# A decoder layer on one core: six of eight block transposes move from TensorE to VectorE and DMA, with a new order of token rows

## The chip, the cores and the metric

One Trainium2 chip, one of its cores. The core has a TensorE (matrix products into PSUM), a VectorE, a ScalarE and a GpSimd, and DMA queues that its engines issue to; SyncE (SP) issues most of the transfers here. The metric is the device time of one execution in microseconds. An execution that was profiled apart from the timed ones gives the profile.

## The reference, cut to what matters

2048 tokens of 512 features go through grouped self-attention against 512 gathered cache rows and the keys of the first sequence, cross attention against an encoder output within each sequence of 64 tokens, and a feed-forward with a low-rank part. After each, the result is added to the tokens and normalised.

```python
# x: (32, 64, 512); 32 query heads, 8 key/value heads, head dimension 128
k_full = concatenate([k_cache[block_idx], k[0]])        # 512 + 64 keys, the same for all tokens
x = layernorm(x + softmax(q @ k_full.T / sqrt(128)) @ v_full @ wo.T)
q = x @ Wq + bq
k, v = split(ctx @ Wkv + bkv)                            # 64 keys in each sequence
x = layernorm(x + softmax(q @ k.T / sqrt(128)) @ v @ Wo + bo)
z = x @ W.T + b
m = sum over e of p[e] * (x @ A[e]) @ B[e]
x = layernorm(x + z + min(0.5 * |z| / (|m| + 1e-6), 1) * m)
```

Everything is float32. In self-attention each token meets the same 576 keys, so neither the order of the tokens nor that of the keys matters there. In cross attention a token must meet the 64 keys of its own sequence.

## The kernel before

**Blocks.** The tokens are cut into four blocks (`NTB`) of 512 (`TB`). A block lives in two forms. `acc[tb]`, 128 partitions by 4 rows (`TPB`) by 512 features, collects the sums and is normalised in place: tokens lie on partitions. `xT[tb]`, 128 partitions by 4 feature groups by 512 tokens, feeds the products: features lie on partitions. `rows` (L113) says which token stands where in `acc`: row j of partition p is token 128 j + p of the block. The columns of `xT` run in token order.

**Turning a block.** Twice an `acc` block has to be turned into an `xT` block, after the first and after the second normalisation. `transpose_rows` (L127) does one row of 128 tokens: four TensorE transposes of 128x128 into one bank of PSUM (L131) and one copy out by ScalarE or VectorE in turn (L133).

**Stages.** (1) Self-attention, a loop over 128 units, with its products, VectorE reductions and 32x32 turns of the weights. At its start the queries of block 0 and `new_keys` (L586, keys and values of the first 64 tokens) come from `xTs[0]`; later groups read a copy of its first 64 columns, `x64`, that GpSimd makes at L812. (2) The key/value stage, a loop over pairs `(gp, tb)` of two key/value heads and a block; each pair has seven products ("steps"). Between steps one closure of the list `fill` runs: the parts of the first normalisation (put there at gp 1) and then `rows_turn`, a row's `transpose_rows` (put there at gp 2). Each pair ends with two stores of keys and values to DRAM. (3) Cross attention, a loop over 32 units `(g, tb)`. Iteration n makes the queries of unit n (seven steps), then `attend(n - 1)`, then the scores of unit n, then the seven steps of the output projection of unit n - 1 (`steps`), with the softmax of unit n between them (`parts`). (4) The feed-forward of a block (`feed_forward`), the first two interleaved with the last units.

**The products of stage 3.** Each product of two 512-wide matrices is done by seven products of halves, some of them of sums of halves. `attend` (L1128) writes its PSUM banks to `oTx`, tokens on the free axis, four copies of 128x256 on ScalarE (L1161) and four on VectorE (L1163). `output_sums` (L262) lets GpSimd form four sums of the halves of `oTx` (L267 to L273). In `project` the first step needs no sum; the second, step 5, needs the sum of L267, the third, step 6, that of L268.

**Order.** TensorE and VectorE follow the order that is written out in stages 2 and 3, GpSimd too in stage 3; VectorE's order is free from the last full unit on. Each engine takes its instructions in order, so an instruction that waits holds back all that stand behind it. SP issues its transfers in one queue, in order as well.

**The end of stage 3.** When a block's last projection is done (g is 7), its normalisation runs (`layernorm_parts` with ScalarE scaling the rows, L169), and `later` holds `transpose_block` (L135), 16 transposes. For blocks 0 and 1 it runs one iteration after that projection, ahead of query step 4 of the last two full units; for blocks 2 and 3 it runs beside the feed-forward. `feed_forward` takes 128 columns of `xT[tb]` at a time as weights (`cols`, L1212), adds to row i of `acc`, normalises it and stores it.

Of the kernel before, what the change touches and what calls it, by code (L numbers as in the profile page):

```python
# [9 lines left out]
F32 = mybir.dt.float32  # L10
I32 = mybir.dt.int32
AF = mybir.ActivationFunctionType
ALU = mybir.AluOpType
# [39 lines left out]
def decoder_layer(  # L53
# [46 lines left out]


    acc = [act.tile([P, TPB, DIM], F32, tag=f"acc{b}", name=f"acc{b}") for b in range(NTB)]
    xT = []
# [9 lines left out]
    def rows(src, tb):  # L113
        return src[tb * TB : (tb + 1) * TB, :].rearrange("(j p) f -> p j f", p=P)

# [19 lines left out]
    def transpose_block(tb, name):  # L135
        for j in range(TPB):
            transpose_rows(acc[tb][:, j, :], xT[tb], j, f"{name}_{tb}_{j}")

    def layernorm(tb, name):
# [344 lines left out]
    with ExitStack() as ph:  # L484
# [81 lines left out]
        def rotate(g, t0=0, t1=NKT):  # L566
# [15 lines left out]
            nc.vector.tensor_tensor(k4[:, :, :, 0], k4[:, :, :, 0], tmp, ALU.add)  # L582

        x64 = kc.tile([P, NC, SEQ], F32, name="x64")

        def new_keys(g):  # L586

            wk, wv = wkv_cur.pop(g)  # L590
            src = xTs[0] if g == 0 else x64
            kTs[g] = kv.tile([P, NKEY], F32, tag="kT", name=f"kT{g}")
            new = bank([P, 1, TB], f"new{g}", "po1")[:, 0, :]
            pk, pv = new[:, :SEQ], new[:, P : 2 * P]
            for c in range(NC):
                nc.tensor.matmul(
                    pk, wk[:, c, :], src[:, c, :SEQ], start=(c == 0), stop=(c == NC - 1),
                    skip_group_check=True,
                )
            for c in range(NC):  # L600
                for i in range(2):
                    nc.tensor.matmul(
                        pv[i * SEQ : (i + 1) * SEQ, :], src[:, c, :SEQ], wv[:, c, :],
                        start=False, stop=(c == NC - 1), skip_group_check=True,
                    )
# [175 lines left out]
        for j in range(NKT):  # L781
            gather_keys(0, j)
        nc.vector.tensor_tensor(t[1], q[0, 1], q[0, 0], sub)
        nc.vector.tensor_tensor(wq0[7], wq0[1], wq0[5], sub)
# [26 lines left out]
        cached_keys(0, "s0")  # L811
        nc.gpsimd.tensor_copy(x64, xTs[0][:, :, :SEQ])  # L812
        nc.vector.tensor_tensor(t[3], q[1, 1], q[0, 1], sub)
# [153 lines left out]
    with ExitStack() as ph:  # L967
# [23 lines left out]
        with ExitStack() as st:  # L991
# [8 lines left out]
            kvw[1] = load_kv_left(1, "wo")  # L1000
            fill, turns = [], [0]

            def rows_turn(src, dst, j, name):
                transpose_rows(src, dst, j, name, f"t{turns[0] % 2}")
                turns[0] += 1

            pairs = [(gp, tb) for gp in range(NKV // 2) for tb in range(NTB)][1:]
            for k, (gp, tb) in enumerate(pairs):
# [3 lines left out]
                if gp == 2:  # L1012
                    fill += [lambda tb=tb, j=j: rows_turn(
                        acc[tb][:, j, :], xT[tb], j, f"x1_{tb}_{j}") for j in range(TPB)]
                tiles = [ke.tile([P, 2, 2, HF], F32, tag=f"c{i}", name=f"c{gp}_{tb}_{i}", bufs=2)
# [112 lines left out]
        def attend(n):  # L1128

            g, tb = units[n]  # L1130
            oTs[n] = output_tiles(f"oTx{g}_{tb}")
            o5 = [o.rearrange("d h (t b q) -> d t b h q", t=TPB, b=2) for o in oTs[n]]
            po = {}
# [19 lines left out]
            for pr in range(2):  # L1153
                for j in range(2):
                    for b in range(2):
                        dst = o5[j][:, 2 * pr : 2 * pr + 2, b, :, :]
                        src = po[pr, b][:, :, j * HF // 2 : (j + 1) * HF // 2].rearrange(
                            "d i (h q) -> d i h q", h=2
                        )
                        if b == 0:  # L1160
                            nc.scalar.activation(dst, src, AF.Identity, bias=bias)  # L1161
                        else:
                            nc.vector.tensor_scalar(dst, src, bias, None, ALU.add)  # L1163
            left = output_sums(oTs.pop(n), f"sox{g}_{tb}", False)
# [3 lines left out]
        def project(n, *steps):  # L1168
# [4 lines left out]
            if steps[-1] == 4:  # L1173
                del pjs[n]
                if g == NKV - 1:
                    stats, scale = layernorm_parts(tb, "x", by_act=True)
                    stats()
                    scales.append(scale)
                    later.append(lambda: transpose_block(tb, "x2"))

# [16 lines left out]
        def feed_forward(tb, between=None):  # L1197
# [60 lines left out]

        ffn_w, next_t = [], {}
        N = len(units)  # L1260
# [21 lines left out]
        for n in range(N + 1):  # L1282
# [127 lines left out]
```

## Time and profile before

| | us |
|---|---|
| three timed runs, median (lowest to highest) | 3056.8 (3054.63 to 3058.08) |
| the profiled execution | 3057.02 |
| its span, first to last instruction | 3055.2 |

| stretch of the span, us | what runs there |
|---|---|
| 0 to 30 | the start: loads, first queries, new keys |
| 30 to about 1870 | self-attention |
| about 1870 to 2042 | keys and values of cross attention |
| 2042 to 2946 | cross attention, 28.3 us a unit |
| 2946 to the end | feed-forward, the last projection among it |

Of the groups of instructions by line and shape, those that the change touches:

| line, engine, what | shape | count | mean, ns |
|---|---|---|---|
| L131 TensorE, transposes | 128x128 | 128 | 275 |
| L133 ScalarE, copies of them | 128x512 | 16 | 591 |
| L133 VectorE, copies of them | 128x512 | 16 | 684 |
| L1161 ScalarE, oTx from pox | 128x256 | 128 | 470 |
| L1163 VectorE, oTx from pox | 128x256 | 128 | 479 |
| L1108 VectorE, 32x32 turns of cross attention's weights | 128x512 | 64 | 686 |
| L1218 TensorE, feed-forward products | 128x512 | 128 | 592 |

A profile is read here by stretches: the totals say which engine is full, the timeline of a stretch says whether that engine has gaps in it and who ends them. Durations of TensorE overlap, since products are pipelined; what one costs is the distance from its start to the start of the next. The timeline gives start, duration, engine, line, operation, the names out<-in, shape and count, and in brackets the idle time before and what ended it. Consecutive instructions of one kind are merged into one row.

### The profile page before, as it was taken

The numbers are of one execution on the slowest core, as the hardware profiler recorded it, in microseconds if no ns is written. First come the engines' busy times: TensorE is split into PE (matmuls) and PEld (weight loads), VectorE is DVE, ScalarE is ACT, GpSimd is POOL, SyncE is SP. The second block draws the span as 40 slices with busy tenths as digits, with TensorE's granted clock in tenths as the row PEclk, the third lists the DMA queues.
The fourth block names the chain that finished last, engine by engine and source line by source line (L and its number), as shares of the span: only waits on it lengthen the run. The fifth ranks groups of instructions, "written<-read, shape, count | busy, mean of one in ns | idle before, by whom it ended". The sixth has DMA issues, their size and how long they took to land.

```text
span 3055.2 us, 42257 instructions
## 1 busy us (share of the span) xinstructions
PE 3021.4 (99%) x14944; PEld 2320.5 (76%) x14944; DVE 2171.4 (71%) x3929; ACT 768.5 (25%) x1776; POOL 944.8 (31%) x774
## 2 busy tenths in 40 slices
PE   8999999999999999999999999999999999999998
PEld 6677777777777777777777769998888888888864
DVE  7787787787777877877877764436666666666677
ACT  2323223222232332223232221211111111111233
POOL 4221321321321321321321223035444444444410
PEclk9999999999999999999999999999999999999999
DMA  5444444444444444444454344231121121121101
GB/s 172 129 132 129 110 115 127 108 113 130 106 125 118 105 127 117 103 128 121 100 130 109 88 122 146 102 113 56 49 66 53 53 65 50 56 62 49 56 28 42
DMA packets 201104, 298.65 MB, mean 98 GB/s; under 512 B 44352, under 2 KB 95040, under 8 KB 200896
## 3 DMA queue, kind: packets, MB, share of 16 engines
q1 hardware_dynamic: 186224, 280.60, 33.7%
q10 hardware_dynamic: 12624, 11.16, 1.3%
q0 software_dynamic: 2048, 4.20, 0.5%
q8 instruction: 120, 1.97, 0.3%
q14 instruction: 88, 0.72, 0.1%
HBM read 107.05 MB, written 20.97 MB: 42 GB/s over the span
## 4 chain that ended last, share of the span: by engine, by line
PE 93%; DVE 3%; DMA 1%; SPq 1%; ACT 1%; issue 1%; POOL 0%; ACTq 0%; DVEq 0%; POOLq 0%
PE po L681 16%; PE s L635 15%; PE sx L1072 2%; PE pox L1143 2%; PE w_2y L296 1%; PE q_3y L296 1%; PE w_0y L296 1%; PE w_3y L296 1%; PE qx_0y L296 1%; PE wx_1y L296 1%; PE wx_0y L296 1%; PE wx_3y L296 1%; PE q_2y L296 1%; PE qx_2y L296 1%; PE qx_1y L296 1%; PE qx_3y L296 1%
## 5 line engine op out<-in xcount | busy, mean ns | idle before, releaser
L643 ACT ACTIVATE p<-s,nmax 128x576 f32<-128x576 f32 x512 | 379.1, 740 | 1246.2 <-DVE nmax L640 1233.9
L635 PE MATMUL s<-kT,qT 128*128 128x288 f32 x2048 | 578.2, 408 | 4.6 <-ACT p L643 3.8
L681 PE MATMUL po<-pT,v 128*128 128x512 f32 (+1 forms) x1280 | 549.4, 603 | 5.6 <-DMA pT<-T 5.6
L635 PEld LDWEIGHTS s<-kT,qT 128*128 128x128 f32 x2048 | 388.2, 190 | 108.0 <-issue 18.2
L640 DVE TENSOR_REDUCE nmax<-s 128x1 f32<-128x576 f32 x512 | 384.1, 750 | 61.5 <-PE s L635 61.5
L661 DVE STREAM_TRANSPOSE T<-p 128x576 f32<-128x576 f32 x512 | 394.2, 770 | 4.4
L681 PEld LDWEIGHTS po<-pT,v 128*128 128x128 f32 (+1 forms) x1280 | 213.4, 189 | 205.2 <-issue 178.8
L653 DVE TENSOR_SCALAR p<-p,den 128x576 f32<-128x576 f32 x512 | 317.0, 619 | 17.9
L652 DVE RECIPROCAL den<-den 128x1 f32<-128x1 f32 x512 | 83.9, 164 | 230.1 <-ACT p L643 219.3
L267 POOL TENSOR_TENSOR so<-oT,oT 128x512 f32<-128x512 f32 x32 | 40.7, 1271 | 551.4 <-ACT oT L704 551.4
L270 POOL TENSOR_TENSOR so<-oT 128x512 f32<-128x512 f32 x32 | 40.7, 1270 | 347.7 <-ACT oT L704 97.3
L267 POOL TENSOR_TENSOR sox<-oTx,oTx 128x512 f32<-128x512 f32 x32 | 40.7, 1273 | 283.9 <-DVE oTx L1163 258.4
L208 POOL TENSOR_TENSOR tx<-xT 128x512 f32<-128x512 f32 x31 | 39.6, 1279 | 206.3 <-PE q_3z L296 64.9
L643 ACT ACTIVATION_READ_ACCUMULATOR p<-s,nmax 128x1 f32 x512 | 98.7, 193 | 0.0
L1255 POOL TENSOR_TENSOR txx<-x1T 128x512 f32<-128x512 f32 x31 | 39.3, 1268 | 188.6 <-PE qx_3z L296 79.4
L1089 ACT ACTIVATE ex<-ex 128x512 f32<-128x512 f32 x64 | 40.4, 631 | 222.0 <-DVE ex L1088 222.0
L1161 ACT ACTIVATE oTx<-pox,bv 128x256 f32<-128x256 f32 x128 | 51.9, 470 | 119.6 <-PE pox L1143 119.6
L1072 PEld LDWEIGHTS sx<-kvx,qTx 128*64 128x64 f32 x2048 | 62.3, 138 | 10.6 <-issue 10.6
L704 ACT COPY oT<-po 128x512 f32<-128x512 f32 x128 | 68.3, 587 | 4.7 <-PE po L681 3.8
L1072 PE MATMUL sx<-kvx,qTx 128*64 128x64 f32 x2048 | 66.7, 224 | 0.0
L1143 PE MATMUL pox<-pTx,kvx 64*128 64x256 f32 x512 | 63.9, 389 | 0.0
L1163 DVE TENSOR_SCALAR oTx<-pox,bv 128x256 f32<-128x256 f32 x128 | 53.6, 479 | 9.5 <-PE pox L1143 9.5
(446 smaller groups left out, 5748.7 us busy)
## 6 DMA issues: line engine op xcount, KB each, us to landing
pT<-T SPq DMA_DIRECT2D x1016, 80.0 KB
pT<-T SPq DMA_DIRECT2D x1008, 64.0 KB
xT<-in_xT SPq DMA_DIRECT2D x31, 1024.0 KB
kvx<-kv SPq DMA_DIRECT2D x32, 512.0 KB
pTx<-Tx SPq DMA_DIRECT2D x256, 64.0 KB
kv<-c SPq DMA_DIRECT2D x30, 512.0 KB
wo<-in_woT SPq DMA_DIRECT2D x32, 256.0 KB
xwq<-in_xwq SPq DMA_DIRECT2D x32, 256.0 KB
```

Source lines behind the costliest of these rows:

```text
L267: nc.gpsimd.tensor_tensor(t[1], a[1, 0], a[1, 1], ALU.add)
L296: nc.tensor.matmul(self.banks[b][:, m, :], self.left[i][:, k, m * P : (m + 1) * P], self.right[i][:, k, :], start=(first and m + k == 0), ...
L635: nc.tensor.matmul(s[:, a, :HALF], qTs[n // REP][:, units[n][2], i * P : (i + 1) * P], kTs[g][:, a * HALF : (a + 1) * HALF], start=True, s ...
L640: nc.vector.tensor_reduce(nmax, s[:, :, :HALF], AX.XY, ALU.max, negate=True)
L643: nc.scalar.activation(p.rearrange("q (a k) -> q a k", a=2), s[:, :, :HALF], AF.Exp, bias=nmax, accum_out=den,)
L652: nc.vector.reciprocal(den, den)
L653: nc.vector.tensor_scalar(p, p, den, None, ALU.mult)
L661: nc.vector.transpose(Ts[n][:, :, i, :], ps_.pop((n, i)).rearrange("q (b k) -> q b k", k=SQ))
L681: nc.tensor.matmul(pos[n].rearrange("d (a q) -> d a q", a=NQD), vs[units[n][0]][rows, v, :], pTs[n // 2][rows, :, chunk, :], skip_group_ch ...
L704: nc.scalar.copy(o[:, i, :].rearrange("d (t a k) -> d a t k", t=TPB, a=NQD), pos.pop(n - 1 + i).rearrange("d (a t k) -> d a t k", a=NQD, t ...
L1072: nc.tensor.matmul(s[b * SEQ : (b + 1) * SEQ, i * REP + h, :], qTs[n][:, h, pr * HF + c0 : pr * HF + c0 + SEQ], kvs[n][:, pr, 0, c0 : c0 + ...
L1143: nc.tensor.matmul(po[pr, b][:, i, :].rearrange("d (h a j) -> d h a j", h=REP, a=2), kvs[n][r, pr, 1, i * HD : (i + 1) * HD], pTs[n][r, :, ...
```

## The change

Four things change together.

*The order of token rows in `acc`.* `rows` now gives row j of partition p the token 4 p + j of the block. The host lays out the input `xT` in the same order (column 128 j + p of a block is token 4 p + j). Self-attention runs in that order throughout. The first 64 tokens are no longer the first 64 columns, so GpSimd gathers `x64` from four runs of 16 columns, ahead of the first `new_keys`, which reads it too.

*The turns.* `turn_rows` lets VectorE turn the 32x32 blocks of a row of tokens into a room, with the four rows j side by side in the last place. `move_rows` then carries the blocks to their partitions with 16 DMAs on SP, 64 KB each, in pieces of 512 bytes. The columns come out in token order, as cross attention needs them. All four blocks are turned so in the key/value stage, one row after each step, the moves after the four, then seven empty places in `fill` before the next block's rows. After cross attention blocks 0 and 1 are turned so, one row at each call of `a_turn`; blocks 2 and 3 keep TensorE's transposes.

*The outputs of `attend`.* They must now be written in the order of `acc`'s rows: column 128 q + 32 t + 16 b + k for token 128 t + 64 b + 4 k + q. A copy of 128x256 becomes two of 128x128, and neighbours in PSUM are written 128 floats apart.

*The feed-forward.* For blocks 0 and 1 `cols` takes every fourth column of the token-ordered `xT`, and the store follows `rows`.

```diff
     def rows(src, tb):
-        return src[tb * TB : (tb + 1) * TB, :].rearrange("(j p) f -> p j f", p=P)
+        return src[tb * TB : (tb + 1) * TB, :].rearrange("(p j) f -> p j f", p=P)
...
+    def turn_rows(src, room, j):
+        nc.vector.transpose(room[:, :, :, j], src.rearrange("p (b f) -> p b f", f=SQ))
+
+    def move_rows(room, dst):
+        blocks = room.rearrange("f (c r) t j -> f r c (t j)", r=NQD)
+        for a in range(NQD):
+            for r in range(NQD):
+                nc.sync.dma_start(
+                    out=dst[r * SQ : (r + 1) * SQ, :, a * P : (a + 1) * P],
+                    in_=blocks[a * SQ : (a + 1) * SQ, r, :, :],
+                )
...
-            src = xTs[0] if g == 0 else x64
...
-                    pk, wk[:, c, :], src[:, c, :SEQ], start=(c == 0), stop=(c == NC - 1),
+                    pk, wk[:, c, :], x64[:, c, :], start=(c == 0), stop=(c == NC - 1),
...
         for j in range(NKT):
             gather_keys(0, j)
+        nc.gpsimd.tensor_copy(
+            x64.rearrange("p c (j k) -> p c j k", j=TPB),
+            xTs[0].rearrange("p c (j k) -> p c j k", j=TPB)[:, :, :, : SEQ // TPB],
+        )
...
-        nc.gpsimd.tensor_copy(x64, xTs[0][:, :, :SEQ])
...
                 if gp == 2:
-                    fill += [lambda tb=tb, j=j: rows_turn(
-                        acc[tb][:, j, :], xT[tb], j, f"x1_{tb}_{j}") for j in range(TPB)]
+                    room = ke.tile([P, DIM // SQ, SQ, TPB], F32, tag="room", name=f"room{tb}")
+                    fill += [lambda tb=tb, j=j, room=room: turn_rows(
+                        acc[tb][:, j, :], room, j) for j in range(TPB)]
+                    fill.append(lambda tb=tb, room=room: move_rows(room, xT[tb]))
+                    fill += [lambda: None] * 7
...
-            o5 = [o.rearrange("d h (t b q) -> d t b h q", t=TPB, b=2) for o in oTs[n]]
+            o5 = [o.rearrange("d h (q t b k) -> d t b h k q", t=TPB, b=2, q=TPB) for o in oTs[n]]
...
-                        dst = o5[j][:, 2 * pr : 2 * pr + 2, b, :, :]
-                        src = po[pr, b][:, :, j * HF // 2 : (j + 1) * HF // 2].rearrange(
-                            "d i (h q) -> d i h q", h=2
-                        )
-                        if b == 0:
-                            nc.scalar.activation(dst, src, AF.Identity, bias=bias)
-                        else:
-                            nc.vector.tensor_scalar(dst, src, bias, None, ALU.add)
+                        for i in range(2):
+                            dst = o5[j][:, 2 * pr + i, b, :, :, :]
+                            src = po[pr, b][:, i, j * HF // 2 : (j + 1) * HF // 2].rearrange(
+                                "d (h k q) -> d h k q", h=2, q=TPB
+                            )
+                            if b == 0:
+                                nc.scalar.activation(dst, src, AF.Identity, bias=bias)
+                            else:
+                                nc.vector.tensor_scalar(dst, src, bias, None, ALU.add)
...
-                    later.append(lambda: transpose_block(tb, "x2"))
+                    if tb < 2:
+                        later.append(lambda: turn_block(tb))
+                    else:
+                        later.append(lambda: transpose_block(tb, "x2"))
+
+        def turn_block(tb):
+            room = sb.tile([P, DIM // SQ, SQ, TPB], F32, tag="room", name=f"room2_{tb}", bufs=1)
+            for j in range(TPB):
+                turns.append(lambda j=j: turn_rows(acc[tb][:, j, :], room, j))
+            turns.append(lambda: move_rows(room, xT[tb]))
+
+        def a_turn():
+            if turns:
+                turns.pop(0)()
+                if len(turns) == 1:
+                    turns.pop(0)()
...
-                cols = slice(i * P, (i + 1) * P)
+                cols = slice(i, None, TPB) if tb < 2 else slice(i * P, (i + 1) * P)
...
-                r0 = tb * TB + i * P
-                nc.sync.dma_start(out=out[r0 : r0 + P, :], in_=a)
+                nc.sync.dma_start(out=rows(out, tb)[:, i, :], in_=a)
...
             if n < N:
+                a_turn()
                 q.step(4)
                 q.read()
+                a_turn()
                 q.step(3)
                 q.read()
+                a_turn()
...
             parts(n, (exponentials, 1), (denominators, 0))
+            a_turn()
             steps(n - 1, 3)
...
-        "xT": g["x"].reshape(NT, DIM).T,
+        "xT": g["x"].reshape(NTB, P, TPB, DIM).transpose(3, 0, 2, 1).reshape(DIM, NT),
```

More of the change, by code (lines that the diff above doesn't have):

```diff
@@ L602, in new_keys @@
                     nc.tensor.matmul(
-                        pv[i * SEQ : (i + 1) * SEQ, :], src[:, c, :SEQ], wv[:, c, :],
+                        pv[i * SEQ : (i + 1) * SEQ, :], x64[:, c, :], wv[:, c, :],
                         start=False, stop=(c == NC - 1), skip_group_check=True,
@@ L1000, in decoder_layer @@
             kvw[1] = load_kv_left(1, "wo")
[L1001 to L1005, printed above, removed]
+            fill = []
             pairs = [(gp, tb) for gp in range(NKV // 2) for tb in range(NTB)][1:]
@@ L1257, in next_tokens @@
                 nc.gpsimd.tensor_tensor(t[3], b[1, 1], b[0, 1], sub)
-        ffn_w, next_t = [], {}
+        ffn_w, next_t, turns = [], {}, []
         N = len(units)
```

## The prediction

> **What bounds the kernel now.** I read the totals of the page first, then the busy time by stage, then the timelines of the three places that the change touches.
>
> ```profile
> PE 3021.4 (99%) x14944; PEld 2320.5 (76%) x14944; DVE 2171.4 (71%) x3929; ACT 768.5 (25%) x1776; POOL 944.8 (31%) x774
> ...
> 1935.80:1992.10 56.30, 56.30 (x403) 53.42 (x403) 18.61 (x28) 12.72 (x32) 5.08 (x4) 1.00 0.26 95
> ...
> 2100.00:2840.00 740.00, 738.82 (x5055) 641.75 (x5054) 478.52 (x837) 113.59 (x238) 341.03 (x269) 1.00 0.20 56
> ```
>
> TensorE is busy 99% of the span (first row). The second row is the stretch of the key/value stage that holds the sixteen turns of x1, the third the middle of cross attention; their columns are stretch, length, then busy time of TensorE, its weight loads, VectorE, ScalarE and GpSimd, clock, DMA share and GB/s. In both TensorE has no gaps while VectorE has half its time free. So a product taken from TensorE is time saved, as long as nobody makes TensorE wait.
>
> **What goes.** Only transposes. In the key/value stage they look like this:
>
> ```profile
> 1937.61 0.60 PE L131 MATMUL x<-ident,acc 128*128 128x128 f32 x4
> 1938.04 1.03 PE L404 MATMUL kv_0y<-te,xwkv 128*128 128x256 f32 x4
> 1938.91 1.05 PE L410 MATMUL kv_0y<-xwkv,te 128*128 128x128 f32 x8
> 1939.80 0.60 PE L131 MATMUL x<-ident,acc 128*128 128x128 f32 x4
> ```
>
> The durations overlap, so read starts: from 1937.61 to 1938.04 four transposes take 0.43 us of TensorE, and a whole step takes 1939.80 - 1938.04 = 1.76 us without them. Sixteen such groups go: 16 x 0.43 = 6.9 us. At the end of cross attention blocks 0 and 1 lose theirs:
>
> ```profile
> 2890.96 0.60 PE L131 MATMUL x<-ident,acc 128*128 128x128 f32 x4
> 2892.05 1.13 PE L131 MATMUL x<-ident,acc 128*128 128x128 f32 x8 [0.49 <-ACT qTx L332]
> 2893.49 0.66 PE L131 MATMUL x<-ident,acc 128*128 128x128 f32 x4 [0.31 <-DVE x1T L133]
> 2893.99 1.89 PE L296 MATMUL qx_2y<-txx,xwq 128*128 128x256 f32 x8
> ```
>
> Here the waits for a bank go with them: 2893.99 - 2890.96 = 3.0 us, and for block 1 by the same starts 2925.87 - 2922.30 = 3.6 us. Together **13.5 us go from the engine that bounds**. The copies of L133 that go with them (ScalarE and VectorE) lie beside products: nothing.
>
> One rule speaks against this: the Trainium skill, "VectorE: DVE Perf Modes", section "Rules for kernel authors", sends a full 128x128 transpose to TensorE when its result may go to PSUM. By the rule the edit should stay undone and gain 0. The rows say why I don't follow it here: four transposes cost 0.43 us of an engine with no gaps, the nearest VectorE row (Tx<-ex, L1108, 128x512) costs 0.69 us of an engine with gaps.
>
> **What comes, in the key/value stage.** Four VectorE turns of 128x512 a block, 0.69 us each by L1108, two if their writes at every fourth float run at half rate. After each step VectorE idles 1 to 3 us, and a bank read now is accumulated into only one or more steps of 1.76 us later: nothing. If that cover went, 16 x 0.69 = 11 us.
> Then 16 moves of 64 KB a block on SP's queue. Nearest row, the moves of cross attention, eight of 64 KB:
>
> ```profile
> 2401.72 4.95 SPq L1122 DMA_DIRECT2D pTx<-Tx  x8
> ```
>
> 0.62 us each, so 16 take 9.9 us, landing some 2 us later: 12 us. Behind them on SP stand the stores of keys and values (two pairs of tiles, so a store may be late by most of a pair's 12.3 us; 10 us stays inside) and the xwq loads, whose own wait is for operands of the running pair. The next block's first turn waits for these landings, since `room` is one buffer; it comes nine steps after the last turn, 9 x 1.76 = 15.8 us. 12 is under 15.8: no wait. If 512-byte pieces, four times as many as in that row, cost double to issue, it is 22 us, and VectorE stops for 6 us, three times, with the bank reads behind it.
>
> **What comes, in every unit of cross attention.** This decides. In `attend` eight copies of 128x256 become sixteen of 128x128, half on each engine, and each writes every 128th float of `oTx` where it wrote runs of 64. GpSimd's first sum (L267) needs all of them, TensorE's second product needs that sum:
>
> ```profile
> 2411.76 2.00 PE L1143 MATMUL pox<-pTx,kvx 64*128 64x256 f32 x16
> ...
> 2413.00 1.62 ACT L1161 ACTIVATE oTx<-pox,bv 128x256 f32<-128x256 f32 x4 [3.75 <-PE pox L1143]
> 2413.04 1.67 DVE L1163 TENSOR_SCALAR oTx<-pox,bv 128x256 f32<-128x256 f32 x4 [0.30 <-PE pox L1143]
> ...
> 2414.85 1.27 POOL L267 TENSOR_TENSOR sox<-oTx,oTx 128x512 f32<-128x512 f32 x1 [11.13 <-DVE oTx L1163]
> ...
> 2417.32 1.70 PEld L296 LDWEIGHTS wx_0z<-xwo,sox 128*128 128x128 f32 x8
> ```
>
> Slack: the last copy ends at 2414.71, the sum starts 0.14 later and is done at 2416.12; the weight load that needs it starts at 2417.32. Allowing 0.1 for the signal, the last copy may be **1.1 us later** before TensorE stands. The first product (2415.70) now needs six copies of each engine, not one; at 0.3 each these end by 2415.2, so it does not decide.
> Price: four copies of 256 in 1.67 with the last lasting 0.48 means a copy every 0.40; rows of 512 follow each other by 0.61 in the same timeline. So 0.81 ns an element and 0.19 fixed; 128 elements cost 0.29. Eight: 7 x 0.29 + 0.37 = 2.4 us against 1.67, 0.75 later. ScalarE's slope is similar and it starts earlier. **0.75 is under 1.1: no cost.**
> The write stride is what this trace does not show. Below, nothing is gained, since no copy gets shorter than its elements. The nearest rows are two VectorE products of the start, one written densely (L578), one at every second float (L579):
>
> ```profile
> 14.50 0.29 DVE L578 TENSOR_TENSOR kq<-kn,sn 128x128 f32<-128x128 f32 x1
> 14.71 0.29 DVE L579 TENSOR_TENSOR kr<-kn,cs 128x128 f32<-128x128 f32 x1
> ```
>
> The same 0.29. Against that stands the Trainium skill, "SBUF — State Buffer", section "Door 1: The DMA port swizzle": SBUF is reached in lines of 16 bytes, an access at full rate needs at least two hits on a line, and each crossing to a new one pays. L579 has two hits a line; the new copies have one. By the rows: 0. By the rule, if the unstated penalty is a doubling of 0.81 ns: copies every 0.40, eight in 3.3 us, 1.6 later. If VectorE starts its first, smaller copy when it is free (2412.74, the end of its query sums L317) rather than at 2413.04, 1.3 later. So TensorE would stand 0.2 to 0.5 us in each of 31 units: 6 to 15 us. I take the rows, and keep the rule for the range.
>
> **What else comes.** Eight turns and 32 moves in the last two full units. A turn there waits for ScalarE's scaling of its rows (L169, done at 2890.6, before the turn's place); behind it on VectorE are the last query sums and the copies of `attend`. The third turn overlaps the copies' start by about 0.3 us: 0.5 us for both units. Block 1's moves go ahead of the last unit's pTx moves on SP and delay them by some 8 us; these were issued by 2947.9 and are read at 2968.57: nothing.
> The feed-forward of blocks 0 and 1 loads weights at every fourth column: 40 loads of 190 ns behind products that follow each other every 0.43 us (eight in 3.43). Doubled it still hides; only at more than twice would each cost, up to 0.3 us, 13 us.
> At the start new_keys(0) reads a copy made by GpSimd, queued between the key gathers (done 8.3) and L577 (starts 11.54): 0.4 us in an idle of 3.2, and TensorE wants it at 14.9: nothing. Token loads and output stores keep their 2 KB pieces.
>
> **Sum.** 3055.2 - 6.9 - 6.6 + 0.5 = 3042.2 us of span. The profiled execution took 3057.0, 1.8 more than its span, and the median is 3056.8, so: **3044 us**, 0.4% faster. A measurement tells 0.2%, 6 us, from no change.
>
> **Rivals.**
> 1. *Strided writes at half rate*: 3044 + 6 to 15 = 3050 to 3059, near no change. For it: the rule. Against: L579.
> 2. *Strided writes much dearer*: same place, the last copy ahead of L267. At three times the element price a copy costs 0.50, eight end 2.4 us later than now, TensorE stands 1.3 us x 31 = 40: 3084; at four times some 3109. It decides for slower once TensorE stands over (13 + 6) / 31 = 0.61 us a unit, that is 2.2 to 2.5 times the price. For it: one hit a line on two engines at once. Against: no row hints at more than the plain rate.
> 3. *The moves are slow*: VectorE waits 6 us for `room`, some 2 are covered, 3 x 4 = 12 back: 3056. For it: 128 pieces in a move, not 32. Against: a 1 MB load of 512 pieces issues in 0.37 us (kind xT<-in_xT at 23.96).
>
> **How the numbers follow.** Forecast 42%, rival 1 22%, rival 2 27%, rival 3 9%. Faster by over 0.2% (below 3051): nearly all of the forecast (41), under half of rival 1 (10), half of rival 3 (5): 56%. Within 0.2%: 11 of rival 1, 4 of rival 3, 1: 16%. Slower: rival 2 and a rest, 28%. The range runs from 3040 (the copies' cover costs nothing at all, and the last units gain a little) to 3070, which takes in rivals 1 and 3 and the near part of rival 2; the forecast's own is 3040 to 3048.
>
> **What will show it.** L131 should count 32; a key/value step should take 1.76 us everywhere. In `attend`, L1163 at 128x128 should last about 0.37 us: near 0.48 means rival 1, above 0.55 rival 2, and then wx_z's load should name GpSimd's sox as its releaser. VectorE idle before `room` released by a DMA means rival 3. The forecast falls if units of cross attention take more than their 28.3 us of now (from 2411.76 to the next unit's pox at 2440.07).

## The result and the profile after

The changed kernel takes **3045.8 us** (median of 7 runs, 3044.6 to 3049.8) against 3056.8 of the kernel before (3054.6 to 3058.1): a ratio of 0.997, with a 95% interval of 0.9961 to 0.9979. The prediction said 3044. The profiled execution took 3049.76 us, with a span of 3048.0.

The totals of the page after, and the busy time of two stretches: the sixteen turns of x1 in the key/value stage, and the middle of cross attention (columns as in the prediction):

```profile
PE 3014.4 (99%) x14848; PEld 2321.9 (76%) x14848; DVE 2200.1 (72%) x4069; ACT 783.8 (26%) x1892; POOL 946.9 (31%) x774
```

```profile
1936.00:1985.25 49.25, 49.25 (x339) 46.37 (x338) 24.42 (x35) 8.43 (x24) 4.78 (x4) 1.00 0.46 143
2100.00:2840.00 740.00, 738.26 (x5003) 641.30 (x5002) 487.27 (x938) 129.57 (x338) 344.10 (x270) 1.00 0.20 57
```

TensorE has 96 instructions less, the 24 groups of four transposes. The stretch of the x1 turns is 49.25 us long where it was 56.30, and TensorE is busy in all of it. VectorE's busy time in it went up from 18.6 to 24.4 us and DMA's share from 0.26 to 0.46, and nobody on TensorE waited for either. In the middle of cross attention TensorE's busy time is 738.26 of 740 us where it was 738.82; these 0.56 us turn up again below.

Distances between the starts of products show where the time went; they are free of whatever happened earlier in the run (pox are the first products of `attend`; unit 2 is the third of the 32):

| from, to | before | after | change | predicted |
|---|---|---|---|---|
| four pairs of the key/value stage with the x1 turns | 56.17 | 49.19 | -6.99 | -6.9 |
| a middle unit of cross attention (pox to pox) | 28.31 | 28.31 | 0 | 0 |
| pox of unit 2 to pox of unit 3 | 29.76 | 30.32 | **+0.56** | 0 |
| pox of unit 28 to pox of unit 29 | 32.77 | 29.74 | -3.03 | -3.0 |
| pox of unit 29 to pox of unit 30 | 31.88 | 28.31 | -3.57 | -3.6 |
| pox of unit 30 to pox of unit 31 | 39.16 | 40.58 | **+1.42** | +0.5 for all of the last units |
| last product to the end of the span | 9.35 | 9.95 | **+0.6** | 0 |

They add up to -11.0 us, and the medians differ by 11.0. One distance is left out of the table because it does not repeat: up to the first product of the key/value stage this execution took 3.7 us more than the profiled one of before. A second profiled run of the same kernel, with 3045.5 us as its median, took 0.35 less than before there, and gave all other rows of the table again to 0.01 us. The experiments below, whose self attention is untouched, scatter from -2.8 to +5.7 us there; the last section shows that much of this goes with the granted clock.

One unit of cross attention after (timeline; columns start, duration, engine, line, operation, shapes, count, and in brackets the idle time before it and what ended it):

```profile
2409.06 2.00 PE L1163 MATMUL pox<-pTx,kvx 64*128 64x256 f32 x16
2410.31 2.30 ACT L1182 ACTIVATE oTx<-pox,bv 128x128 f32<-128x128 f32 x8 [3.75 <-PE pox L1163]
2410.34 2.26 DVE L1184 TENSOR_SCALAR oTx<-pox,bv 128x128 f32<-128x128 f32 x8 [0.30 <-PE pox L1163]
2412.74 1.27 POOL L283 TENSOR_TENSOR sox<-oTx,oTx 128x512 f32<-128x512 f32 x1 [12.02 <-ACT oTx L1182]
2414.62 1.70 PEld L312 LDWEIGHTS wx_0z<-xwo,sox 128*128 128x128 f32 x8
```

Eight copies on VectorE now take 2.26 us where four took 1.67, so GpSimd's sum starts 3.68 us after the first pox where it started 3.09. The weight load that needs the sum still starts 5.56 us after the first pox, as before (2417.32 - 2411.76), with no idle time. The copies became later by 0.59 us and TensorE didn't notice.

With one exception, the row of unit 2 to 3. TensorE there, in before and in after:

```profile
2146.38 1.99 PE L296 MATMUL qx_0y<-txx,xwq 128*128 128x256 f32 x8 [1.18 <-POOL xwq L203]
```

```profile
2143.68 1.99 PE L312 MATMUL qx_0y<-txx,xwq 128*128 128x256 f32 x8 [1.74 <-POOL xwq L219]
```

In this unit GpSimd has the sums of `sox`, then the bias rows of `acc`, then a new set of query weights, one behind the other without a pause: 2130.28 to 2146.4 in before. TensorE waited for the end of that chain already, and a chain that begins 0.59 us later ends as much later. It is the one place where the copies' delay is paid.

The end of cross attention after, on TensorE:

```profile
2886.53 1.89 PE L312 MATMUL qx_2x<-x1T,xwq 128*128 128x256 f32 x8
2888.26 1.89 PE L312 MATMUL qx_2y<-txx,xwq 128*128 128x256 f32 x8
...
2920.12 0.70 PE L1163 MATMUL pox<-pTx,kvx 64*128 64x256 f32 x2
2921.53 1.96 PE L1163 MATMUL pox<-pTx,kvx 64*128 64x256 f32 x14 [0.71 <-DMA pTx<-Tx]
```

The transposes between the two qx_2 groups are gone. The last row is new: in unit 30 pox stops after two products and waits for a DMA. The queue of SP and VectorE show why:

```profile
2904.21 10.68 SPq L150 DMA_DIRECT2D x1T<-room  x16
2915.01 5.00 SPq L1141 DMA_DIRECT2D pTx<-Tx  x8
```

```profile
2912.91 1.30 DVE L1127 STREAM_TRANSPOSE Tx<-ex 128x512 f32<-128x512 f32 x2 [0.20 <-DMA x1T<-room]
```

The moves of pTx stand behind the sixteen moves of block 0, which end at 2914.9. The second turn of Tx itself ends only at 2914.2, so even with an empty queue the moves that need it could have begun just 0.8 us earlier. Two things are late together, in an iteration of which TensorE now saves 3.6 us.

### The profile page after: what moved, and what is told of

Its sections match the earlier page's. It is cut to its first block, busy times and chain, and to the rows that moved or that the text cites. A ratio compares the mean times of both kernels' runs of the same rounds, so it can differ in the third digit from the quotient of the medians.

```text
span 3048.0 us, 42453 instructions
## 1 busy us (share of the span) xinstructions
PE 3014.4 (99%) x14848; PEld 2321.9 (76%) x14848; DVE 2200.1 (72%) x4069; ACT 783.8 (26%) x1892; POOL 946.9 (31%) x774
## 4 chain that ended last, share of the span: by engine, by line
PE 94%; DVE 2%; SPq 1%; DMA 1%; issue 1%; ACT 1%; POOL 0%; ACTq 0%; DVEq 0%; POOLq 0%
PE po L697 16%; PE s L651 15%; PE sx L1091 2%; PE pox L1163 2%; PE w_2y L312 1%; PE q_3y L312 1%; PE w_0y L312 1%; PE w_3y L312 1%; PE q_2y L312 1%; PE qx_0y L312 1%; PE wx_0y L312 1%; PE wx_3y L312 1%; PE qx_2y L312 1%; PE qx_1y L312 1%; PE wx_1y L312 1%; PE w_1y L312 1%
## 5 line engine op out<-in xcount | busy, mean ns | idle before, releaser
L1182 ACT ACTIVATE oTx<-pox,bv 128x128 f32<-128x128 f32 x256 | 73.7, 486 | 117.6 <-PE pox L1163 117.6
L1108 ACT ACTIVATE ex<-ex 128x512 f32<-128x512 f32 x64 | 40.4, 631 | 201.7 <-DVE ex L1107 201.7
L1184 DVE TENSOR_SCALAR oTx<-pox,bv 128x128 f32<-128x128 f32 x256 | 72.6, 422 | 8.5 <-PE pox L1163 8.5
```

## The experiments

Theory A, the prediction's: the gain is TensorE's removed transposes and nothing else; the copies' stride costs nothing. Against it stand the prediction's rivals (the stride slows the copies, the moves stop VectorE), and, for the stride, two readings of why it is free: it costs nothing at all, or (Theory W) it costs write time that lies beside something else. Each experiment changes one thing of the kernel after, or of before where the text says so.

### Each half of the change alone

x2 back on TensorE, so that only the key/value stage is changed:

```diff
-                    if tb < 2:
+                    if tb < 0:
                         later.append(lambda: turn_block(tb))
...
-                cols = slice(i, None, TPB) if tb < 2 else slice(i * P, (i + 1) * P)
+                cols = slice(i * P, (i + 1) * P)
```

> Only the key/value stage keeps the new turns; blocks 0 and 1 are transposed by TensorE again after cross attention, and the rest is as in the changed kernel. My theory (what is saved is TensorE's own time, and nothing else moves): the last units get their 3.0 and 3.6 us back and lose the 1.4 us stall that the changed kernel has ahead of its unit 30, so 5.2 us slower than the changed kernel, about 3051. The rival that the turns after cross attention cost as much as they save (their moves and VectorE's turns in the way) expects no difference from the changed kernel, 3046. Key/value stage: 6.9 us shorter than before under both.

3051.2 us (3049.2 to 3054.0), ratio 0.9985, interval 0.9978 to 0.9991. The key/value pairs keep their -6.99 us, the last units are those of before.

x1 back on TensorE, its copies written to the new column order:

```diff
-        eng(dst[:, :, j * P : (j + 1) * P], pt)
+        eng(dst[:, :, j::TPB] if apart else dst[:, :, j * P : (j + 1) * P], pt)
...
-                    fill += [lambda tb=tb, j=j, room=room: turn_rows(
-                        acc[tb][:, j, :], room, j) for j in range(TPB)]
-                    fill.append(lambda tb=tb, room=room: move_rows(room, xT[tb]))
-
-                    fill += [lambda: None] * 7
+                    fill += [lambda tb=tb, j=j: rows_turn(
+                        acc[tb][:, j, :], xT[tb], j, f"x1_{tb}_{j}") for j in range(TPB)]
```

> Only the blocks after cross attention keep the new turns; x1 is transposed by TensorE again, with its copies out of PSUM written at every fourth float. My theory: the 6.9 us of the key/value stage come back, about 3053. The rival that the key/value stage gains by something else than its transposes (stores or loads that start earlier) expects less than that. The copies, 128x512 at 16 bytes apart: if such a stride alone halves the rate, 1100 to 1150 ns each like the new turns (1100); if only the transposing instruction pays, near the 591 and 684 of the dense copies.

3053.1 us (3050.6 to 3057.6), ratio 0.9994, interval 0.9985 to 1.0002. The kernel after is 5.4 us under the first of these and 7.3 under the second. By the table, the last units should give 3.03 + 3.57 - 1.42 = 5.2 and the key/value stage 7.0: the two halves add up.

### The copies: stride or number?

In before, the copies of `attend` cut in two, still written in runs (the number without the stride):

```diff
-                        dst = o5[j][:, 2 * pr : 2 * pr + 2, b, :, :]
...
+                        for i in range(2):
+                            dst = o5[j][:, 2 * pr + i, b, :, :]
```

> The kernel before, with the copies of attend cut in two but written densely as before. My theory: no change of time (3057), as the last copy may be 1.1 us later; it ends about 0.6 us later than before. The rival that a stride of 512 bytes costs something on the copies expects these dense ones to be clearly shorter than the 422 and 486 ns of the strided ones and to follow each other in less than 0.26 us; my theory expects the same spacing of 0.26. It also tells whether self-attention's 3.7 us more in the changed kernel's profile are chance: by chance this kernel's self-attention can lie anywhere within some 4 us of before's.

3055.3 us, ratio 0.9999, interval 0.9991 to 1.0007. Twice the number of copies costs nothing that the measurement can tell. (GpSimd's sum starts 0.49 us later after pox; unit 2 to 3 takes 0.49 us more, and the first unit, whose copies end 0.93 us later than before, 0.55.) The groups by shape (columns: busy time and mean ns of one, then idle time before them) of this kernel and of the kernel after give the price of the stride:

```profile
L1162 ACT ACTIVATE oTx<-pox,bv 128x128 f32<-128x128 f32 x256 | 69.6, 382 | 119.8 <-PE pox L1143 119.8
L1164 DVE TENSOR_SCALAR oTx<-pox,bv 128x128 f32<-128x128 f32 x256 | 69.4, 343 | 10.0 <-PE pox L1143 10.0
```

```profile
L1182 ACT ACTIVATE oTx<-pox,bv 128x128 f32<-128x128 f32 x256 | 73.7, 486 | 117.6 <-PE pox L1163 117.6
L1184 DVE TENSOR_SCALAR oTx<-pox,bv 128x128 f32<-128x128 f32 x256 | 72.6, 422 | 8.5 <-PE pox L1163 8.5
```

One copy lasts 422 ns with the stride and 343 without, yet the busy time, which counts overlapping instructions once, grew only from 69.4 to 72.6. The starts of VectorE's copies in one unit, in us after the first pox, say why:

| copies | starts | end of the last |
|---|---|---|
| before, four of 256, in runs | 1.28 1.68 2.07 2.47 | 2.95 |
| eight of 128, in runs | 1.28 1.55 1.81 2.06 2.32 2.58 2.84 3.10 | 3.44 |
| after, eight of 128, every 128th float | 1.28 1.56 1.82 2.08 2.34 2.60 2.86 3.11 | 3.54 |

With or without the stride a copy of 128 starts every 0.26 us. Each lasts 0.08 us longer, and that time lies beside the next one: only the last copy's counts.

To test that reading, before's own copies of 256, written eight floats apart:

```diff
-            o5 = [o.rearrange("d h (t b q) -> d t b h q", t=TPB, b=2) for o in oTs[n]]
+            o5 = [o.rearrange("d h (q t b) -> d t b h q", t=TPB, b=2) for o in oTs[n]]
```

> The kernel before, with its four copies of 128x256 on each engine written 8 floats apart instead of in runs of 64; that permutes the tokens of a block, and the output is not the reference's. Theory W (a write that is far apart takes twice as long, but runs beside the fixed part of an instruction, so that a copy of 128 elements hides it and one of 256 does not): copies last about 0.68 us, follow each other every 0.46 to 0.50 us instead of 0.40, and the last ends 0.4 us later than before, which stays inside the slack: 3056. Theory P (PSUM is the slower side, so the write costs nothing at any width): every 0.40 as before.

3055.7 us, ratio 1.0, interval 0.9991 to 1.001; its groups by shape:

```profile
L1161 ACT ACTIVATE oTx<-pox,bv 128x256 f32<-128x256 f32 x128 | 70.1, 715 | 119.5 <-PE pox L1143 119.5
L1163 DVE TENSOR_SCALAR oTx<-pox,bv 128x256 f32<-128x256 f32 x128 | 69.7, 666 | 9.5 <-PE pox L1143 9.5
```

666 ns where before has 479, and now the starts move too: 1.28, 1.80, 2.29, 2.79, one every 0.50 us where it was 0.40. That speaks for Theory W: by estimate from these starts, a strided copy needs 0.50 / 256 = 1.95 ns an element where a dense one grows by (0.40 - 0.26) / 128 = 1.1. At that price 128 elements need 0.25 us, which just fits into the 0.26 that even a dense copy of 128 takes from start to start. The strides differ, 32 bytes here and 512 in the kernel after, and copies of 256 at 512 bytes were not run; that the price is the same at both is supported by the durations alone: from 128 elements at 512 bytes (422 ns) to 256 at 32 (666) they grow by 1.9 ns an element. The time of the kernel stays, since the last copy ends 3.44 us after pox, inside the slack (GpSimd's sum is 0.50 later, and unit 2 to 3 takes 0.50 more).

How much slack is there? The copies of after cut once more, to sixteen of 64 on each engine:

```diff
+                            for h in range(2):
-                            if b == 0:
-                                nc.scalar.activation(dst, src, AF.Identity, bias=bias)
+                                if b == 0:
+                                    nc.scalar.activation(
+                                        dst[:, h], src[:, h], AF.Identity, bias=bias
...
```

> The changed kernel with each copy of attend cut in two once more, 16 of 128x64 on each engine. At 0.20 us a copy the last would end some 4.7 us after the unit's first pox product, 0.6 past the point up to which I count it as hidden. My theory (the last copy releases GpSimd's first sum and that the second projection product): each of 31 units 0.6 us longer, 28.9 us, 19 us in all, about 3065, and the weight load of wx_z names GpSimd's sum as its releaser. The rival that the copies are not on any path that TensorE waits for expects 28.3 us a unit and 3046.

3061.0 us (3058.4 to 3064.2), ratio 1.0017, interval 1.001 to 1.0024: slower than before, as expected, by a smaller amount. A unit takes 28.72 us, 0.41 more, and unit 2 to 3 takes 1.87 more than before (GpSimd's sum is 1.67 later after pox), 1.3 above after. From the first product of the key/value stage to the end the profile is 14.1 us longer than that of after, of the 15.2 us by which the medians differ. The other 1.1 us are not accounted for. Its timeline:

```profile
2411.79 2.00 PE L1163 MATMUL pox<-pTx,kvx 64*128 64x256 f32 x16
...
2413.04 3.44 ACT L1183 ACTIVATE oTx<-pox,bv 128x64 f32<-128x64 f32 x16 [3.75 <-PE pox L1163]
...
2416.55 1.26 POOL L283 TENSOR_TENSOR sox<-oTx,oTx 128x512 f32<-128x512 f32 x1 [13.11 <-ACT oTx L1183]
...
2417.86 1.59 PEld L312 LDWEIGHTS wx_0z<-xwo,sox 128*128 128x128 f32 x8 [0.54 <-POOL sox L283]
```

This is the path that the prediction drew, and here it binds: the copies end 4.69 us after the first pox, GpSimd's sum follows, and the weight load of wx_0z stands 0.54 us and names the sum as its releaser. The last copy is 4.69 - 2.95 = 1.74 us later than before and costs 0.41, so the slack is 1.3 us. VectorE's copies of 64 start every 0.19 us, which is what the slope of dense copies gives (0.26 - 64 x 0.0011): here too the stride adds nothing to the distance of starts.

### The turn's own stride

The turns of x1 and x2 written in runs of 32 floats, which puts the tokens' columns in another order:

```diff
-        nc.vector.transpose(room[:, :, :, j], src.rearrange("p (b f) -> p b f", f=SQ))
+        nc.vector.transpose(
+            room.rearrange("p b t j -> p b (t j)")[:, :, j * SQ : (j + 1) * SQ], ...
```

> The changed kernel with the turns written in runs of 32 floats instead of at every fourth float; that leaves the columns of the turned blocks out of token order, and the output is not the reference's. If the stride makes the new turns slow, they fall from 1100 ns to the 686 of the other turns of that size; if it is their source or shape, they stay. No change of the stages either way, since VectorE is not what they wait for: key/value stage 7.0 us shorter than before.

A single run, 3047.3 us; no interval can be given. The turns, first of after, then of this kernel (groups by shape):

```profile
L143 DVE STREAM_TRANSPOSE room<-acc 128x512 f32<-128x512 f32 x24 | 25.5, 1100 | 0.1
```

```profile
L143 DVE STREAM_TRANSPOSE room<-acc 128x512 f32<-128x512 f32 x24 | 16.2, 693 | 0.1
```

1100 ns with floats 16 bytes apart, 693 in runs, and the key/value pairs lose the same 6.99 us in both: 0.4 us a turn, all of it hidden there. In the last units it is not: pox of unit 30 to 31 is 0.94 us longer than before in this run and 1.42 in after. With the shorter turns the block moves are done sooner, and the first move of pTx is issued 5.5 us ahead of that pox (2918.22 - 2912.70), where after has 5.1 (2920.12 - 2915.01). TensorE's weight loads feel such a stride as well: those of the feed-forward last 249 ns on average after, and 190 before; the 64 of 128 that read every fourth column last 308, the others 190. The products stay at the same distance.

### The gap of seven steps

The empty steps between a block's moves and the next block's turns taken out:

```diff
-                    fill += [lambda: None] * 7
```

> The changed kernel without the seven empty places behind a block's moves, so that the next block's first turn comes one step into the next pair. My theory (one room: the turn waits until all 16 moves of the block ahead have landed, 11 us of issuing and 1.5 of landing after its last turn): VectorE stands some 9 us before each of three blocks' first turn with the bank reads of the products behind it, of which 2 to 3 us are covered; TensorE stands 7 us three times, 20 us in all, about 3066, and the trace shows VectorE's turn released by a DMA. The rival that the moves are done so early that the gap is for nothing expects 3046.

3071.6 us (3070.6 to 3077.8), ratio 1.0053, interval 1.0036 to 1.007: 16 us slower than before. VectorE and TensorE in the second block's pair (timelines):

```profile
1963.40 1.08 DVE L143 STREAM_TRANSPOSE room<-acc 128x512 f32<-128x512 f32 x1 [8.67 <-DMA x1T<-room]
1964.33 0.67 DVE L437 TENSOR_TENSOR c<-kv_1y,c 128x512 f32<-128x512 f32 x1
```

```profile
1958.22 1.05 PE L426 MATMUL kv_1z<-xwkv,te 128*128 128x128 f32 x8
1965.05 2.07 PE L420 MATMUL kv_1y<-te,xwkv 128*128 128x256 f32 x4 [5.78 <-DVE c L437]
1966.92 1.92 PE L426 MATMUL kv_1y<-xwkv,te 128*128 128x128 f32 x8
```

This is rival 3 made real: the turn waits 8.67 us for the one `room`, the bank read L437 stands behind it on VectorE, and TensorE stands 5.78 us for the bank. Three of the pairs take 20.4 us where 12.3 is normal: 8.1 each, 24.3 in all, where 7 each was expected. The rest of the 8.1 is the clock, in the busy time by stretch (the third number from the end is the granted clock):

```profile
1959.00:1965.00 6.00, 0.27 (x3) 0.08 (x1) 1.60 (x3) 0.00 (x0) 0.00 (x0) 0.79 0.65 216
1965.00:1969.00 4.00, 3.95 (x13) 3.55 (x14) 1.95 (x3) 0.00 (x0) 0.00 (x0) 0.50 0.11 41
```

After the stand the granted clock is 0.50 for four microseconds, and half a step takes 1.87 us (1965.05 to 1966.92) where 0.87 is normal.

### The stall of unit 30

Two causes were suspected: the sixteen moves ahead of pTx on SP, and the late turn of Tx on VectorE. The moves put behind those of pTx, with two rooms:

```diff
-            turns.append(lambda: move_rows(room, xT[tb]))
+            moves.append(lambda: move_rows(room, xT[tb]))
...
                     move(n)
+                while moves and not turns:
+                    moves.pop(0)()
```

> The changed kernel, with the moves of blocks 0 and 1 after cross attention issued behind that unit's pTx moves instead of ahead of them, and two rooms there so that the next block's turns need not wait. In the changed kernel TensorE stands 1.4 us in attend of unit 30 for pTx, whose moves stand behind 16 block moves on SP. Theory A (SP's queue is the cause): the stall falls to about 0.7 us, what remains being the late turn of Tx on VectorE; 0.7 us faster than the changed kernel. Theory B (the turn of Tx alone is late, because the iteration has become 3.6 us shorter): the stall stays at 1.4.

3046.1 us, ratio 0.9965, interval 0.9951 to 0.9978. pox of unit 30 to 31 is 0.58 longer than before instead of 1.42. The turn of Tx put ahead of the last projection step and the statistics:

```diff
-                steps(n - 1, 4)
+                ahead = units[n - 1][0] == NKV - 1
+                if not ahead:
+                    steps(n - 1, 4)
                 parts(n, (turn, 0), (turn, 1))
...
                     move(n)
+                if ahead:
+                    steps(n - 1, 4)
```

> The changed kernel, with VectorE's turn of Tx and the pTx moves put ahead of the last projection step and the normalisation's statistics in the last units (moves of blocks as in the changed kernel). Theory A: the 1.2 us stall of TensorE in the queries of unit 30 (it waits for a bank read that stands behind the statistics and the turn) goes, but pTx of unit 30 still stands behind the block moves on SP, which now are needed 1.2 us earlier, so the stall in attend grows to about 2 us: 0 to 0.7 us faster in all. Theory B: both stalls go, 2.6 us faster.

3045.0 us, ratio 0.9964, interval 0.995 to 0.9977: units 28 to 29 gain another 0.59 (-3.62), unit 30 to 31 stays 1.52 longer. Both edits together:

> Both of these edits together: the turn of Tx and its moves first, the block moves behind them. Theory A and B: both stalls go, 2.6 us less than the changed kernel in the last units, about 3043 by median.

3045.3 us, ratio 0.9966, interval 0.9952 to 0.9979. The stall is not gone, it has moved. TensorE at the end of cross attention in this kernel:

```profile
2884.22 1.97 PE L312 MATMUL qx_2y<-txx,xwq 128*128 128x256 f32 x8 [0.59 <-DVE rstd_x L181]
...
2919.61 2.00 PE L1163 MATMUL pox<-pTx,kvx 64*128 64x256 f32 x16
...
2923.83 1.96 PE L312 MATMUL wx_2x<-xwo,oTx 128*128 128x256 f32 x8 [0.21 <-DVE oTx L1184]
...
2929.83 1.53 PE L312 MATMUL wx_2z<-xwo,sox 128*128 128x256 f32 x6 [0.42 <-DVE acc L381]
```

pox runs through, but wx_2x now waits for a copy and wx_2z for a bank read, both on VectorE, and the query product still waits 0.59 for statistics. Unit 30 to 31 is 1.07 longer than before; over the last units the pair of edits is 0.94 us better than after, where 2.6 was expected. Moving work about on VectorE there trades one wait for another. No median of these three can be told from that of the kernel after, which ran beside them:

> The changed kernel once more. If the 3.7 us that its first profile shows more than before in self-attention are chance, this profile has another number there, while the key/value stage (7.0 us shorter), the last units (3.0 and 3.6 us shorter, one stall of 1.4) and the units of 28.3 us repeat to 0.1 us. If they belong to the new order of tokens, they repeat as well. Median 3046.

3045.5 us (3044.1 to 3048.1), ratio 0.9966, interval 0.9952 to 0.998. So no version here beats the kernel after by more than the measurement can tell.

## Why the prediction was right

**TensorE's removed time is the gain.** The terms 6.9, 3.0 and 3.6 us were measured as 6.99, 3.03 and 3.57, and each half alone gives its share. The sum was -13.0 us of span, the measured one -11.0; the 2.0 between them are the missed terms below. Subtracting start times around the removed products, not their durations, is what made these exact: the row has 0.60 us, the distance 0.43. One reading was loose, but no term rested on it: in the middle of cross attention VectorE is busy for 478.52 of 740 us, so a third of its time is free, not half.

**The row against the rule of transposes.** The Trainium skill, "VectorE: DVE Perf Modes", section "Rules for kernel authors", would have kept the turns on TensorE. The measured turn is 1100 ns on VectorE against 0.43 us on TensorE, so VectorE is even worse at it than the 0.69 that the prediction took from the row of L1108, and the move still gains. What decides is which engine has gaps. (The prediction named half rate as the other end; what came is 1.6 times the time of that row.)

**The moves.** Priced at 0.62 us each, 9.9 for sixteen; they take up to 11.5 in the key/value stage and 10.7 in block 0 of x2. With the landing (1.7 us in the run without the gap, from 1961.68, the end of the moves' issue, to the turn at 1963.40) that is still under the 15.8 us of nine steps, and no turn of x1 waits more than 0.06 us in the kernel after. The experiment without the gap shows the other side of the same inequality.

**The copies.** Predicted 0.75 us later, inside 1.1 us of slack; measured 0.59 inside 1.3, in thirty of thirty-one units. The outcome was as forecast, but the reason was incomplete. The prediction set the row of L579 (a stride of two floats is free) against the rule of the Trainium skill, "SBUF — State Buffer", section "Door 1: The DMA port swizzle", as if one of them had to be wrong. Both stand: L579 has the two hits a line that the rule asks for, so it could not tell what one hit costs, and that taking its side came out right was in part luck. Where there is one hit, the runs agree with the rule: the turn at 1100 against 693 ns, and the strided copies of x1 in the second experiment, 128x512 at 16 bytes apart, at 1076 (VectorE) and 1104 ns (ScalarE) where before has 684 to 687 and 582 to 591:

```profile
L134 ACT COPY x1T<-x 128x512 f32<-128x512 f32 x8 | 8.8, 1104 | 9.6 <-PE x L132 9.6
L134 DVE COPY x1T<-x 128x512 f32<-128x512 f32 x8 | 8.6, 1076 | 0.0
```

It costs next to nothing in `attend` because a copy of 128 elements is short: its slower writes still end within the time from one start to the next. Rival 1 fell on exactly that term, "copies every 0.40": they come every 0.26. The sign named for it, a duration near 0.48, was the wrong one to read: 0.42 and 0.49 were measured, with no cost. The starts decide.

**Three terms were missed**, together 2.1 us net of the 0.5 that was allowed for. "No cost" for the copies was read from one unit's slack and applied to all; in unit 2 GpSimd had none, and the trace of before shows it, in the 1.18 us for which TensorE waits there: +0.56. The third turn overlapping the copies was put at 0.5 us for the last units; measured is +1.42 on one distance, from another cause. The prediction looked at block 1's moves ahead of the last unit's pTx and found them harmless; it did not look at block 0's ahead of unit 30's, where TensorE had lost 3.6 us of its iteration and the turn of Tx had not moved with it. And the output stores "keep their 2 KB pieces", but the rows of one store now lie 8 KB apart. The last scaling on VectorE, in before and in after:

```profile
3051.51 0.55 DVE L185 TENSOR_SCALAR acc<-acc,mv_f,rstd_f 128x512 f32<-128x512 f32 x1
```

```profile
3043.66 0.55 DVE L201 TENSOR_SCALAR acc<-acc,mv_f,rstd_f 128x512 f32<-128x512 f32 x1
```

From its end to the end of the span, which holds only the last store, are 3.2 us before and 3.8 after. The ten profiles of kernels that store rows 8 KB apart have 3.5 to 3.8 there, the three with adjoining rows (before, and before with its copies cut or spread) 3.2. That speaks for the spacing of the rows, which was not tried by itself.

The term of the feed-forward's weight loads was sized wrongly as well, without effect: the trace has 80 loads at every fourth column where the prediction counts 40, and they last 308 ns, less than the doubled 190 for which it still found them hidden.

## What to carry to other kernels

Where one engine has no gaps, price a move off it by the starts around the removed instructions, and price what the move adds against the slack of the chain that it feeds, not by whether the new engine is slower at it. Judge a strided write by the distance from one start to the next: here copies of 128 elements hid it and copies of 256 did not. Slack is read from every unit that differs, not from a typical one: a wait that is already there passes on each delay in full. And when the bounding engine becomes earlier at a place, look there for every transfer and turn that it reads next, and for the queue that they stand in: they were in time only for the old pace.

## What was not expected of the hardware

- Writing fp32 32 bytes apart took VectorE an estimated 1.95 ns an element (copies of 256 on 128 partitions, one every 0.50 us), runs 1.1. At 16 bytes apart, whole instructions of 512 elements go from 684 to 693 up to 1076 to 1100 ns, on ScalarE from 582 to 591 up to 1104. Copies of 128 elements start every 0.26 us on VectorE either way.
- After a stand of 5.8 us TensorE runs at a granted clock of 0.50 for some four microseconds, here about 2 us on top of each stall. The Trainium skill, "TensorE: Matmul & The Clock Gate", section "Part 1: The HAM clock gate", says that an idle window of about 3.4 us halves the clock and a busy one restores it. The restoring agrees; a full window of standing is not needed: in the profiled run of the kernel with Tx turned first, a stand of 1.98 us (the wait for `xwq` in unit 2 to 3) was followed by a clock of 0.56 over the next 3.9 us, with 1.00 again behind them, and eight products took 3.61 us where after has 1.99:

```profile
2137.68 3.61 PE L312 MATMUL qx_0y<-txx,xwq 128*128 128x256 f32 x8 [1.98 <-POOL xwq L219]
```

  The run without the gap stands 1.99 us there and loses as much. After has a stand of 1.74 at that place and keeps a clock of 1.00. The length of a stand alone does not settle it: near the end of self attention the kernel with x2 back on TensorE stands for 2.12 us, that with Tx turned first for 2.27, and both keep 1.00.
- Self attention, the same code in all these kernels but for the gather of `x64` at its start, differed by up to 8 us between their profiled executions (-2.8 to +5.7 against before), more than several of the effects above. Much of it goes with the granted clock. The four executions with no stretch at 0.50 ahead of the first key/value product reach it after 1813.0 to 1816.1 us, the three with the longest, 13.6 us in all, after 1819.4 to 1821.4. Before has 6.8 us of such stretches, the repeat of after 3.4, and the profiled execution of after 13.6, in these two places (columns as above):

```profile
57.20:64.00 6.80, 5.50 (x9) 2.87 (x10) 5.14 (x10) 2.26 (x5) 0.00 (x0) 0.50 0.38 102
1791.20:1798.00 6.80, 5.88 (x9) 3.17 (x10) 3.46 (x7) 0.83 (x2) 0.65 (x1) 0.50 0.61 154
```

  At half clock 6.8 us more cost an estimated 3.4 of the 3.7 us by which after is later than before there. Only distances within a stage could tell effects as small as those above.
